# Two attention blocks over images: layer 1's first convolution taken in halves twice, and the projection put ahead of it

## The chip, the cores and the metric

The kernel runs on one core of a Trainium2 chip, all in float32. The metric is the device time of one launch in microseconds (us). The kernel before was timed in three runs; a further run was profiled. TensorE (PE in the profile) multiplies matrices, VectorE (DVE) and GpSimd (POOL) do elementwise work, ScalarE (ACT) does exponentials, copies and additions of a bias, and SyncE (SP) starts nearly all transfers (DMAs). On-chip data lie in SBUF; matrix products land in banks of PSUM.

## The reference

Input x has 8 images of 512 channels and 32 x 32 points (1024 tokens). Two layers follow each other, each adding its result to its input:

```
layer 0:  h = group_norm(x)                     (32 groups)
          q, k, v = W_qkv h + b_qkv             (8 heads of 64 channels)
          a = softmax(q k^T / 8) v              per head, over 1024 tokens
          x = x + W_proj a + b_proj             (called "projection", p)
layer 1:  h = group_norm(x)                     (8 groups)
          out = softmax((q h)(k h)^T / sqrt(512)) (v h)    one head
          x = x + W_p out + b_p
```

In layer 1 the kernel folds weights: the scores become g times h with g = m h plus a bias (m joins the weights of query and key), and the output becomes z = h times (value and projection weights joined), so layer 1 is g, scores, z, values. Dividing by the sum of exponentials is done afterwards, by a row of reciprocals r.

## The kernel before, in words

Everything is done image by image. An image of the steady loop (b from 1 to 6) passes these stages: layer 0's attention of image b; g of image b-1 and the projection of image b; layer 1's scores, z and values of image b-1; then v, k and q of image b+1. The matmuls stay in the order in which the program issues them, so the order of calls in the main loop is the order on TensorE. On the other engines a scheduler orders the instructions, except where `tc.keep_in_program_order` pins one.

**Products by halves.** `wino` splits both operands into halves and takes 7 products in place of 8, with sums of the factors made before (`left_sums` for the left operand, `right_sums` for the right one, where the image stands; `image_factors` calls the latter, 8 subtractions of 128x512). Each of the seven is a step of 4 matmuls of 128x128 by 512 columns (two parts of the output by two parts of the input channels; the profile counts each matmul twice, so it shows x8). `ORDER` is 1, 5, 2, 6, 7, 3, 4, while `middle` sets the order of the four steps between the first and the last two. Steps 1 and 2 add up in PSUM bank a, 6, 7 and 4 in bank b, 5 and 3 in bank c. The last two steps of a product are put in the list `tail`, and `finish()` issues them once the next product's first step has been issued; `hooks` are calls after the steps, and `background` is a list of small jobs of which each step takes some.

**Halves twice.** `conv2` applies the same splitting once more: 49 products of 128x128 by 256 columns instead of 28 by 512. Its operand needs `inner_factors`: 28 subtractions of 128x256 on GpSimd (line 411). Its weights are kept as `sums2_k` and `sums2_q` by `keep2`, which needs four additions of 128x896 on GpSimd (line 306), and are loaded in two parts. In before k and q of layer 0 are made by `conv2`; g (weights m), p, v and z by `wino`.

**Attention of layer 0.** `attention0` takes 8 blocks, each a pair of heads (`hp`, four of them) and a half of the tokens (`tb`). A block makes eight tiles of scores (`sc`), exponentials of them on ScalarE (`e`, line 594), their running sum on VectorE (lines 596 and 598), the values (`av`), then the sums over tokens by TensorE and their reciprocals by VectorE (`reciprocals`, line 559); a transfer spreads these over the partitions as r, and GpSimd multiplies (line 615). Only the last block's multiplication (line 617) is left for later, as `scaled`, on VectorE. `extra` holds 16 lists of jobs, two for each block: one between scores and values, one after the values. The images' normalisation (`h`, by ScalarE) is put there.

**g and the projection.** `layer1_scores` makes the factors of h on VectorE (lines 170 to 173), then g; `projection` follows, whose `residual` (lines 845 and 847) adds the bias and the input x, and puts statistics for layer 1's normalisation in the background. After the projection x is written to a spill buffer in DRAM. The attention's result a needs factors too: eight subtractions by `image_factors`, once the last block is scaled.

The following lines are those that a sentence can't say well: in before, the last block and the order of the main loop are

```
if (hp, tb) != (KC - 1, 1):
    nc.gpsimd.tensor_tensor(dst, dst, r, ALU.mult)
else:
    scaled = lambda dst=dst, r=r: nc.vector.tensor_mul(dst, dst, r)
...
hf, gf = layer1_scores(b - 1, h, ends)
norm1 = projection(b, af, xt)
```

Of the kernel before, what the change touches and what calls it, by code (L numbers as in the profile page):

```python
# [9 lines left out]
F32 = mybir.dt.float32  # L10
# [19 lines left out]
def two_attention_blocks_kernel(  # L30
# [145 lines left out]
    def main_path(ctx):  # L176
# [116 lines left out]

        wdram2 = {n: dram.tile([P, 7, 7, P], F32, name=f"sums2_{n}") for n in "qk"}

# [13 lines left out]

        twice = [("k", 0), ("k", 1), ("q", 0), ("q", 1)]  # L310
        uses = ["v", "p", *twice] if B > 1 else ["p"]
        for b in range(1, B):
            uses += ["m", "p", "z"] + (["v", *twice] if b + 1 < B else [])
        uses += ["m", "z"]
        loaded = []

        def load_weight():
            if uses:
                n = uses.pop(0)
                t = wpool.tile([P, 7 * C], F32, tag="w", name=f"w_{n[0]}_{len(uses)}")  # L320
                if n in twice:
                    t = t.rearrange("p (i j m) -> p i j m", i=4, j=7)
                    i = n[1]
                    t = t[:, : 4 - i]
                    nc.sync.dma_start(t, wdram2[n[0]][:, 4 * i : 4 + 3 * i])
                else:
                    t = t.rearrange("p (i k m) -> p i k m", i=7, k=2)
                    nc.sync.dma_start(t, wdram[n])
                loaded.append((n, t))
# [9 lines left out]

        def image_factors(h, uid):  # L340

            tiles = [pair_tile(f"t{i}_{uid}") for i in (1, 2, 4)]
            halves = lambda t: (t[:, :HT], t[:, HT:])
            return right_sums(
                [halves(t) for t in h[:2]], [halves(t) for t in h[2:]],
                [lambda j, t=t: t[:, j, :] for t in tiles], nc.vector.tensor_sub,
            )
# [67 lines left out]

        def conv2(n, f, bias, name, hooks=(), late=None):

# [121 lines left out]
            pair(2, (7,), [(1, 0)], [(0, 1)], [lambda: biased_half(1, 1)])  # L539
            last = [lambda: biased_half(0, 1), lambda: biased_half(1, 0)]  # L540
            if late is not None:
                late += last
                last = []
            pair(3, (3, 4), [(0, 1), (1, 0)], [(0, 1), (1, 0)], [load_weight, *last])
            return out


        def reciprocals(total, uid, across):

            sums = acc_tile(f"sums_{uid}")[:, : 2 * P].rearrange("p (a b) -> p a b", a=2)
            for i in range(4):
                matmul(sums[ts(i, 32), :, :], ones[:, :32], total[:, :, ts(i, P)], start=True, stop=True)
            rc = rpool.tile([P, 2, P], F32, tag="rc", name=f"rc_{uid}")
            nc.vector.reciprocal(rc, sums)  # L559
            nc.vector.tensor_tensor(low_recs, low_recs, rc, ALU.min)  # L560
            nc.gpsimd.tensor_tensor(all_recs, all_recs, rc, ALU.add)  # L561
            rows = rowpool.tile([2, 4, P], F32, tag="rows", name=f"rows_{uid}")
            nc.sync.dma_start(rows.rearrange("j i n -> i j n"), rc[0:P:32, :, :])
            if across:
                r = pair_tile(f"r_{uid}")
                for j in range(2):
                    row = rows[j : j + 1].rearrange("j i n -> j (i n)")
                    nc.sync.dma_start(r[:, j, :], row.to_broadcast([P, HT]))
            else:
                r = rpool.tile([P, HT], F32, tag="r", name=f"r_{uid}")  # L570
                for j in range(2):
                    row = rows[j : j + 1].rearrange("j i n -> j (i n)")
                    nc.sync.dma_start(r[ts(j, 64), :], row.to_broadcast([64, HT]))
            return r


        def attention0(b, q, k, v, extra):
            a = channel_tiles(f"a0_{b}")
            n = 0
            for hp in range(KC):  # L580
                for tb in range(2):
                    uid = f"0_{b}_{hp}_{tb}"
# [29 lines left out]
                    nc.scalar.copy(dst, av)  # L612
                    r = reciprocals(total, uid, False)
                    if (hp, tb) != (KC - 1, 1):
                        nc.gpsimd.tensor_tensor(dst, dst, r, ALU.mult)  # L615
                    else:
                        scaled = lambda dst=dst, r=r: nc.vector.tensor_mul(dst, dst, r)

            assert not extra
            return a, scaled  # L620

# [130 lines left out]
        def prologue():  # L752
# [44 lines left out]
            later = []  # L797
            for n in "pmz":
                t, steps = prepare(n)
                later.append(steps)  # L800
                later.append([lambda n=n, t=t: keep(n, t), load_weight])
            later.append([
# [3 lines left out]
            ])  # L806
            return v, q, k, norm1, later

        psum_pools("first", 2)
        v, q, k, norm0, later = prologue()  # L810

# [21 lines left out]

        def attention_steps(a, scaled, b):
            af, steps = image_factors(a, f"a_{b}")
            return af, [[], [scaled, lambda: background.extend(steps)]]

        def projection(b, af, xt):

            norm = GroupNorm(1, f"1_{b}")  # L840

            def residual(i, r, c, ps, u):
                oc = 2 * r + i
                xh = xt[oc][:, ts(c, HT)]
                nc.vector.scalar_tensor_tensor(xh, ps, obias[0][:, oc : oc + 1], xh, ALU.add, ALU.add)
                if u is not None:
                    nc.vector.tensor_add(xh, xh, u)  # L847
                background.append(lambda: norm.half_stats(oc, c, xh))

                if c == 1 - r:  # L850
                    background.append(lambda: norm.end_stats(oc))

            def store():
                spills[b] = spool.tile([KC, P, T], F32, tag="spill", name=f"spill_{b}")
                for c in range(KC):
                    nc.sync.dma_start(spills[b][c], xt[c])

            by_channel(weight("p"), af, f"p_{b}", residual, after=[load_weight, store])
            return norm

        def norm_hooks(norm, uid):
            return [
                [], [], [all_background], [lambda: norm.group_mean(acc_tile(f"gmean_{uid}")[:, :KC])],
                [lambda: norm.affine(acc_tile(f"gvar_{uid}")[:, :KC])],
            ]
# [25 lines left out]

        def layer1_scores(b, h, hooks):
            hf, steps = image_factors(h, f"h1_{b}")
            background.extend(steps)
            g = conv(
                weight("m"), hf, ubias, f"g1_{b}", middle=(2, 5, 6, 7), hooks=hooks, back=4,
                after=[load_weight, lambda: background.extend(gsteps)],
            )
            stiles = [pair_tile(f"sg{i}_{b}") for i in (1, 2, 4)]
# [4 lines left out]
            )  # L904
            return hf, gf

        def layer1_rest(b, hf, gf, hooks, ahead):
            e, total, ef = scores1(b, gf, hf, f"1_{b}", hooks)
            state = {}
# [18 lines left out]
        for b in range(B):  # L928
# [11 lines left out]
            for i, f in enumerate(applies):  # L940
                extra[2 * i + 3].append(f)
            if b > 0:
                extra[0] += late
            psum_pools(f"attention_{b}", 1)
            a, scaled = attention0(b, q, k, v, extra)
            psum_pools(f"products_{b}", 2)
            xt = [load_x(b, c, "x") for c in range(KC)]
            af, ends = attention_steps(a, scaled, b)
            if b > 0:
                hf, gf = layer1_scores(b - 1, h, ends)  # L950
                norm1 = projection(b, af, xt)
                if b + 1 < B:
# [8 lines left out]
            elif B > 1:  # L961
                v, f, norm0 = values(1, h, ends)
                norm1 = projection(0, af, xt)
                q, k, late = keys_and_queries(1, f, norm0, norm_hooks(norm1, "1_0")[1:])
            else:
                for f in sum(ends, []):
                    f()
                all_background()
                norm1 = projection(0, af, xt)
                finish()  # L970
                for f in sum(norm_hooks(norm1, "1_0"), []):
                    f()
                h, loads, applies = begun(load_again, norm1, 0, "h1")
                for f in loads + applies:
                    f()
        hf, gf = layer1_scores(B - 1, h, ())
        layer1_rest(B - 1, hf, gf, (), ())
# [196 lines left out]
```

## Time and profile before

| what | value |
|---|---|
| times of three runs | 2908.39, 2902.1, 2906.97 us (median 2906.97) |
| the profiled run | 2902.66 us, span of the core 2900.9 us, granted clock of TensorE 0.999 |
| busy: TensorE, VectorE, ScalarE, GpSimd | 2886.5, 1932.5, 872.2, 468.9 us |
| one block of attention (from 773.34 to 787.99) | 14.65 us |
| a step of 128x512 products in g or p | about 3.44 us |

A line of a timeline gives the start, the time from there to the end of a run of like instructions, the engine, the line of the code, the operation, output and inputs by their names with sizes, and how many (x). In brackets stands how long the engine was idle before it and which instruction released it. A line of a group gives the number of instructions, then their total busy time in us and the mean of one in ns, and then the idle time before them. Busy TensorE means no more than that matmuls were in flight: their ends are modelled.

### The profile page before, as it was taken

Reading aid. Unit: us, or ns where it says so; the run is one execution under the profiler, and the core shown is the slowest. Engines: PE = TensorE matmul, PEld = TensorE weight load, DVE = VectorE, ACT = ScalarE, POOL = GpSimd, SP = SyncE. Lnnn points to the kernel's source line nnn. Section 1 sums busy time; section 2 is a strip of 40 time slices with the busy share of each in tenths; the row PEclk is TensorE's granted clock in tenths of the full one; section 3 lists DMA queues with packets and bytes.
Section 4 is the critical chain, followed back from the end, with each engine's and each line's share of the span. In section 5 each row is a group of like instructions: output and inputs, shape, how many; then the busy total and the mean of one; then the engine's idle time right before and its main releaser. Section 6 shows DMA issues by size and latency. Waiting matters only on the chain.

```text
span 2900.9 us, 29024 instructions
## 1 busy us (share of the span) xinstructions
PE 2886.5 (100%) x10838; PEld 1500.3 (52%) x10838; DVE 1932.5 (67%) x2613; ACT 872.2 (30%) x1117; POOL 468.9 (16%) x525
## 2 busy tenths in 40 slices
PE   9999999999999999999999999999999999999999
PEld 5435634565345653457434574346733458334544
DVE  5488687567766578665776557866577665776555
ACT  1251451214512055121551115411163112631110
POOL 3023210032200321003210122102121031110000
PEclk9999999999999999999999999999999999999999
DMA  8433403123122231222212232122411224011201
GB/s 277 153 137 109 159 19 110 72 103 132 34 98 92 95 113 48 84 92 105 107 48 80 92 135 77 48 80 99 154 55 44 80 103 151 26 59 65 94 1 66
DMA packets 84186, 267.97 MB, mean 92 GB/s; under 512 B 10371, under 2 KB 29891, under 8 KB 75974
## 3 DMA queue, kind: packets, MB, share of 16 engines
q1 hardware_dynamic: 83622, 265.89, 25.5%
q8 instruction: 87, 1.43, 0.2%
q14 instruction: 61, 0.50, 0.1%
q10 hardware_dynamic: 416, 0.16, 0.0%
HBM read 216.30 MB, written 49.72 MB: 92 GB/s over the span
## 4 chain that ended last, share of the span: by engine, by line
PE 98%; issue 1%; DVE 0%; POOL 0%; ACT 0%; DVEq 0%; POOLq 0%
PE sc L67 16%; PE av L67 15%; PE psb_sc L67 6%; PE psb_av L67 6%; PE psa_av L67 4%; PE psa_sc L67 4%; PE psc_av L67 4%; PE psc_sc L67 4%; PE psb_g L67 3%; PE psb_z L67 3%; PE psb_p L67 3%; PE psb_v L67 3%; PE psb_k L67 3%; PE psb_q L67 2%; PE psa_g L67 2%; PE psa_v L67 2%
## 5 line engine op out<-in xcount | busy, mean ns | idle before, releaser
L598 DVE TENSOR_TENSOR sum<-sum,e 128x1024 f32<-128x1024 f32 x384 | 518.6, 1351 | 40.4 <-DVE sum L598 0.5
L594 ACT ACTIVATE e<-sc 128x1024 f32<-128x1024 f32 x512 | 476.8, 1052 | 72.9 <-PE sc L67 72.9
L67 PE MATMUL sc<-q,k 64*128 64x512 f32 x2048 | 458.3, 596 | 0.0
L67 PE MATMUL av<-e,v 128*64 128x512 f32 x2048 | 453.6, 595 | 0.0
L67 PEld LDWEIGHTS sc<-q,k 64*128 64x128 f32 x2048 | 192.3, 186 | 239.3 <-ACT e L594 110.3
L67 PEld LDWEIGHTS av<-e,v 128*64 128x64 f32 x2048 | 141.4, 137 | 304.3 <-issue 302.3
L561 POOL TENSOR_TENSOR all_recs<-all_recs,rc 128x256 f32<-128x256 f32 x72 | 64.4, 894 | 880.2 <-DVE rc L559 880.2
L559 DVE RECIPROCAL rc<-sums 128x256 f32<-128x256 f32 x72 | 126.4, 1756 | 89.7 <-PE sums L67 87.4
L615 POOL TENSOR_TENSOR a<-a,r 128x512 f32<-128x512 f32 x56 | 109.5, 1955 | 274.0 <-DMA r<-rows 247.5
L646 ACT ACTIVATE e<-e 128x512 f32<-128x512 f32 x96 | 60.5, 630 | 232.7 <-DVE e L645 232.7
L612 ACT COPY a<-av 128x512 f32<-128x512 f32 x64 | 37.4, 585 | 305.2 <-PE av L67 305.2
L596 DVE TENSOR_TENSOR sum<-e,e 128x1024 f32<-128x1024 f32 x64 | 78.6, 1228 | 59.8 <-ACT e L594 59.8
L67 PE MATMUL psa_sc<-g,h 128*128 128x512 f32 x256 | 115.7, 594 | 0.0
L67 PE MATMUL psa_av<-e,z 128*128 128x512 f32 x256 | 113.3, 595 | 0.0
L128 POOL TENSOR_TENSOR rstd<-ve,mhalf 128x4 f32<-128x4 f32 x16 | 16.7, 1043 | 499.9 <-DVE ve L126 499.9
L140 ACT ACTIVATE h<-h,b,s 128x1024 f32<-128x1024 f32 x62 | 78.5, 1270 | 60.7 <-DMA h<-in_x 48.0
L67 PEld LDWEIGHTS psa_sc<-g,h 128*128 128x128 f32 x256 | 48.1, 190 | 57.9 <-issue 56.2
L67 PEld LDWEIGHTS psa_av<-e,z 128*128 128x128 f32 x256 | 48.0, 190 | 57.3 <-issue 55.4
L67 PE MATMUL psb_k<-inner_h,w_k 128*128 128x256 f32 x294 | 75.4, 383 | 0.0
L67 PE MATMUL psb_q<-inner_h,w_q 128*128 128x256 f32 x294 | 74.9, 383 | 0.0
L249 ACT COPY t_sc<-psa_sc 128x512 f32<-128x512 f32 x32 | 18.7, 585 | 181.7 <-DVE x L847 152.4
L444 POOL TENSOR_TENSOR k<-k,k 128x256 f32<-128x256 f32 x28 | 20.0, 727 | 291.0 <-DVE u_k L439 291.0
(304 smaller groups left out, 4580.8 us busy)
## 6 DMA issues: line engine op xcount, KB each, us to landing
x<-in_x SPq DMA_DIRECT2D x36, 512.0 KB
h<-in_x SPq DMA_DIRECT2D x32, 512.0 KB
r<-rows SPq DMA_DIRECT2D x128, 128.0 KB
spill<-x SPq DMA_DIRECT2D x32, 512.0 KB
h<-spill SPq DMA_DIRECT2D x32, 512.0 KB
x<-spill SPq DMA_DIRECT2D x32, 512.0 KB
out<-x SPq DMA_DIRECT2D x64, 256.0 KB
w_p<-sums_p SPq DMA_DIRECT2D x8, 1792.0 KB
```

Source lines behind the costliest of these rows:

```text
L67: tc.keep_in_program_order(nc.tensor.matmul(*args, **kw))
L140: tc.keep_in_program_order(nc.scalar.activation(dst, src, AF.Identity, bias=b, scale=s))
L249: nc.scalar.copy(t1[i], ps["a", i])
L444: nc.gpsimd.tensor_tensor(d, x, y, ALU.add)
L559: nc.vector.reciprocal(rc, sums)
L561: nc.gpsimd.tensor_tensor(all_recs, all_recs, rc, ALU.add)
L594: nc.scalar.activation(e, sc, AF.Exp, scale=(C // 8) ** -0.5)
L596: nc.vector.tensor_add(total, es[0], e)
L598: nc.vector.tensor_add(total, total, e)
L612: nc.scalar.copy(dst, av)
L615: nc.gpsimd.tensor_tensor(dst, dst, r, ALU.mult)
L646: nc.scalar.activation(dst, dst, AF.Exp, scale=scale)
```

## The change

It has six parts.

1. g of images 0 to 6 is made by `conv2` (49 products of 256 columns), as k and q are. Its weights are loaded in two parts from `sums2_m`; four more additions of 128x896 on GpSimd make them, once, in the first attention. The last image's g stays with `wino`.
2. In the steady loop the projection goes ahead of g, with its middle steps in the order 5, 6, 7, 2. The scaled multiplication and the last two factors of a (t4) go in a hook of its third step. The first image has no g at that place.
3. The last pair of heads takes its second half of tokens first, so that the last block is the first half of a's last tile, which only products 2 and 4 of the projection read. The transfers of its reciprocals are issued by ScalarE, and the multiplication by them is pinned on VectorE.
4. The eight factors of h for g are made during the attention (two each in `extra` 9 to 12), six of a's eight factors are pinned there as well (`extra` 13 and 15), and h is normalised in `extra` 1, 3, 5 and 7 in place of 3, 5, 7 and 9. The 28 inner factors of h are issued after the attention on GpSimd.
5. The residual is pinned on VectorE; its statistics go in the background only within g; the hooks of the normalisation come one step earlier; `finish()` puts g's last steps before the scores' first; and `conv2` adds the bias of the half (1,0) before that of (0,1).
6. In the prologue the weights are prepared in the order p, z, m, and one load of weights moves.

The core of the diff:

```diff
-        wdram2 = {n: dram.tile([P, 7, 7, P], F32, name=f"sums2_{n}") for n in "qk"}
+        wdram2 = {n: dram.tile([P, 7, 7, P], F32, name=f"sums2_{n}") for n in "qkm"}
...
-            last = [lambda: biased_half(0, 1), lambda: biased_half(1, 0)]
+            last = [lambda: biased_half(1, 0), lambda: biased_half(0, 1)]
...
-                for tb in range(2):
+                for tb in (0, 1) if hp < KC - 1 else (1, 0):
...
-                    r = reciprocals(total, uid, False)
-                    if (hp, tb) != (KC - 1, 1):
+                    last = (hp, tb) == (KC - 1, 0)
+                    r = reciprocals(total, uid, False, nc.scalar if last else nc.sync)
+                    if not last:
                         nc.gpsimd.tensor_tensor(dst, dst, r, ALU.mult)
                     else:
-                        scaled = lambda dst=dst, r=r: nc.vector.tensor_mul(dst, dst, r)
+                        scaled = lambda dst=dst, r=r: tc.keep_in_program_order(nc.vector.tensor_mul(dst, dst, r))
...
-            for n in "pmz":
+            for n in "pzm":
                 t, steps = prepare(n)
                 later.append(steps)
-                later.append([lambda n=n, t=t: keep(n, t), load_weight])
+                later.append([lambda n=n, t=t: keep(n, t)])
+            later[1].append(load_weight)
...
-            return v, q, k, norm1, later
+            return v, q, k, norm1, later, lambda: (keep2("m", t), load_weight())
...
-                nc.vector.scalar_tensor_tensor(xh, ps, obias[0][:, oc : oc + 1], xh, ALU.add, ALU.add)
+                tc.keep_in_program_order(
+                    nc.vector.scalar_tensor_tensor(xh, ps, obias[0][:, oc : oc + 1], xh, ALU.add, ALU.add)
+                )
                 if u is not None:
                     nc.vector.tensor_add(xh, xh, u)
-                background.append(lambda: norm.half_stats(oc, c, xh))
+                stats.append(lambda: norm.half_stats(oc, c, xh))
...
-            g = conv(
-                weight("m"), hf, ubias, f"g1_{b}", middle=(2, 5, 6, 7), hooks=hooks, back=4,
-                after=[load_weight, lambda: background.extend(gsteps)],
-            )
+            after = [lambda: background.extend(gsteps)]
+            if inner:
+                g = conv2("m", inner, ubias, f"g1_{b}", hooks, after)
+            else:
+                g = conv(weight("m"), hf, ubias, f"g1_{b}", middle=(2, 5, 6, 7), back=4, after=[load_weight, *after])
...
+            finish()
             e, total, ef = scores1(b, gf, hf, f"1_{b}", hooks)
...
             for i, f in enumerate(applies):
-                extra[2 * i + 3].append(f)
+                extra[2 * i + 1].append(f)
+            a = channel_tiles(f"a0_{b}")
+            af, steps = image_factors(a, f"a_{b}", lambda *t: tc.keep_in_program_order(nc.vector.tensor_sub(*t)))
+            extra[13] += steps[:2]
+            extra[15] += steps[2:6]
             if b > 0:
                 extra[0] += late
+                hf, sums = image_factors(h, f"h1_{b - 1}")
+                for i in range(4):
+                    extra[9 + i] += sums[2 * i : 2 * i + 2]
...
             if b > 0:
-                hf, gf = layer1_scores(b - 1, h, ends)
-                norm1 = projection(b, af, xt)
+                inner, sums2 = inner_factors(hf, f"h1_{b - 1}")
+                for f in sums2:
+                    f()
+                hooks = [[], [], [scaled, *steps[6:]]]
+                norm1, stats = projection(b, af, xt, middle=(5, 6, 7, 2), hooks=hooks)
+                gf = layer1_scores(b - 1, hf, inner, [[], [lambda: background.extend(stats)]])
...
             elif B > 1:
-                v, f, norm0 = values(1, h, ends)
-                norm1 = projection(0, af, xt)
+                more_later()
+                v, f, norm0 = values(1, h, [[], [scaled, lambda: background.extend(steps[6:])]])
+                norm1, stats = projection(0, af, xt)
+                load_weight()
...
```

## The prediction

> **What bounds the kernel now.** I read the busy shares first, then the chain that ended last, then the form groups of the products, and last the timelines of one steady image.
>
> ```profile
> span 2900.9 us, 29024 instructions
> ...
> PE 2886.5 (100%) x10838; PEld 1500.3 (52%) x10838; DVE 1932.5 (67%) x2613; ACT 872.2 (30%) x1117; POOL 468.9 (16%) x525
> ...
> PE 98%; issue 1%; DVE 0%; POOL 0%; ACT 0%; DVEq 0%; POOLq 0%
> ```
>
> TensorE is the bound: 98% of the chain. A change pays only by fewer matmul cycles, or by removing the few waits that are left; and any other engine that comes late shows up one for one. So the prices are those of matmuls, and how late VectorE may be. A block of layer 0's attention starts at 773.34:
>
> ```profile
> 773.34 7.14 PE L67 MATMUL sc<-q,k 64*128 64x512 f32 x32
> ...
> 777.87 8.75 DVE L598 TENSOR_TENSOR sum<-sum,e 128x1024 f32<-128x1024 f32 x6
> 780.67 2.21 POOL L615 TENSOR_TENSOR a<-a,r 128x512 f32<-128x512 f32 x1 [4.34 <-DMA r<-rows]
> ...
> 787.42 0.64 PE L67 MATMUL sums<-sum,ones 128*32 128x256 f32 x8
> ...
> 788.18 1.76 DVE L559 RECIPROCAL rc<-sums 128x256 f32<-128x256 f32 x1 [1.56 <-PE sums L67]
> ```
>
> The reader is to see the margin: a block takes 787.99 - 773.34 = 14.65 us, the last add of its exponentials ends at 777.87 + 8.75 = 786.62, and the sums that need it start at 787.42. VectorE is early by about 0.75 us, no more. Where GpSimd's L615 runs, one of the adds takes 2.1 instead of 1.2 us (six adds in 8.75 us, against 7.87 in block 2 of the first attention, where no L615 runs beside them).
>
> The products of g and p in the steady image:
>
> ```profile
> 813.05 3.60 PE L67 MATMUL psb_g<-t_h,w_m 128*128 128x512 f32 x8
> 816.64 3.79 PE L67 MATMUL psb_g<-h,w_m 128*128 128x512 f32 x8
> 820.26 3.60 PE L67 MATMUL psa_p<-a,w_p 128*128 128x512 f32 x8
> 823.70 3.60 PE L67 MATMUL psb_g<-t_h,w_m 128*128 128x512 f32 x8
> ...
> 1005.53 1.03 PE L67 MATMUL psc_k<-inner_h,w_k 128*128 128x256 f32 x4
> 1006.40 1.03 PE L67 MATMUL psb_k<-inner_h,w_k 128*128 128x256 f32 x4
> ```
>
> Undisturbed steps start 823.70 - 820.26 = 3.44 us apart (four products, so 0.858 each at 512 columns), those in halves twice 0.87 for two products (0.431 to 0.435 each at 256). The second and third lines come 0.16 and 0.19 late: the waits in the present order.
>
> **What the Trainium skill says.** "SBUF — State Buffer", section "Who interferes with whom": a VectorE instruction with two SBUF inputs contends with a GpSimd instruction that reads SBUF, the pair of ports is an exclusive lock, and the loser blocks for a whole instruction; one with at most one SBUF input isn't touched. The trace agrees:
>
> ```profile
> 955.72 0.69 DVE L238 TENSOR_TENSOR w_av<-psb_av,t_av 128x512 f32<-128x512 f32 x1 [2.74 <-PE psb_av L67]
> ...
> 957.17 1.22 DVE L686 TENSOR_TENSOR o<-o,r 128x512 f32<-128x512 f32 x1
> 958.42 1.10 DVE L688 SCALAR_TENSOR_TENSOR x<-o,obias,x 128x512 f32<-128x512 f32 x1
> ```
>
> ```profile
> 957.80 1.17 POOL L411 TENSOR_TENSOR inner_h<-h 128x256 f32<-128x256 f32 x1
> ```
>
> L238 reads one input from PSUM and keeps its 0.69; L686 and L688 read two from SBUF while GpSimd forms factors, and take 1.22 and 1.10 instead of 0.69 and 0.75. So a VectorE instruction of that kind costs up to 0.5 us more whenever factors are formed beside it. The change puts 28 more of those on GpSimd per image.
>
> **Part 1, g in halves twice (images 0 to 6).** Removed: 28 products x 0.858 = 24.03 us. Added: 49 x 0.431 = 21.12. Gain 2.91 per image, 20.4 in all. k and q in the same form take 43.5 together against 42.2 by count, so each carries about 0.6 of waits of its own (0.1 to 0.2 at each of the later pairs); g's wait at its start is counted in part 2, so +0.5 here. The two weight loads of m instead of one lie on SP behind loads that are as large and are needed as late as k's; nothing waits for k's now, so nothing here.
>
> **Part 2, projection ahead of g.** The waits of the present mixture go: 0.16 + 0.19 + about 0.1 at g's start = -0.45. New: g's first product uses bank a, which the projection's second product fills last, and must wait until the residual (L845) has read it. Take T0 as the end of the attention's last sums. The projection's five steps end at T0 + 5 x 3.433 = 17.17. VectorE has in its fixed order ahead of that residual: last a*r (it can start at T0+11.2, behind two L238 adds of the product that ends at T0+10.3), two t4 subtractions, two L238, an L845, an L847, another L845, a statistics instruction, the other L847. At the spacings of 811 to 845 (0.60 for independent tensor_tensor, 0.66 for L845, 0.72 if it needs the one before) the residual ends at T0+18.06: TensorE waits 0.95 by the queue alone. GpSimd starts the 28 factor subtractions when the last scores are done (about T0-4.6; the pinned order lets them go no earlier), 0.68 each = 19 us, and 3 more with VectorE in the way: it is busy to T0+17 or beyond. a*r and the two L847 read two SBUF tiles: 3 x 0.25 = 0.75. I take 0.95 + 0.75 = 1.7; the ends are 0 (VectorE catches up) and 2.7 (every contested one, t4 as well, loses 0.35 to 0.5). The statistics that stand behind it in the queue are waited for by nobody for another 20 us.
>
> **Part 3, the last block with a's half that only two products need.** The scaled multiplication in before, at 811.68, was 9 us after the last sums; in the changed kernel T0+11.2 against a need at T0+13.7, so it is off the path with the 0.69 it takes; ACT issues its three transfers (rows and two broadcasts) instead of SP, between a's copy and the first copy of the projection, which has 3.4 us to spare. Nothing.
>
> **Part 4, factors spread over the attention.** VectorE gets two h subtractions in each of blocks 4, 5 and 6 between the sixth and the seventh add. In before the last add ends 13.28 after the block's start. Two subtractions of 0.60 come ahead of it, and as they need no add before them, two pauses of 0.1 between dependent adds (1.33 apart, 1.23 long) fall away: 13.28 + 1.2 - 0.2 = 14.28. The sums must start at 14.0 to keep the pace: 0.28 late per block, 0.84 per image (ends 0 and 1.2). Block 7 has GpSimd's factors beside its last three adds: it ends at 13.9 to 14.04, so 0 to 0.5; I take 0. The four a subtractions after it push its reciprocal to T0+1.7, which part 3's T0+11.2 includes. h's applies on ACT come one half-block earlier; their loads were issued by 676 and the first apply is due after 694. Nothing.
>
> **Part 5, statistics and the tail of g.** g's tail runs before the scores; ACT has two pairs of biased halves ahead of the first copy of the scores: four times 0.62 to 0.72, of which TensorE sees about 0.27 (ends 0 and 0.6).
>
> Per image: -2.91 + 0.5 - 0.45 + 1.7 + 0.84 + 0.27 = -0.05; times 7, -0.4.
>
> **Part 6, once.** m's four weight sums run on GpSimd in the first attention, from about 164.5: the same form in before,
>
> ```profile
> L306 POOL TENSOR_TENSOR prepare_k<-prepare_k 128x896 f32<-128x896 f32 x4 | 8.2, 2079 | 5.3 <-DMA sums_q<-prepare_q 5.3
> ```
>
> takes 2.08 us, read from SBUF throughout, against VectorE's chain of dependent adds with two SBUF inputs and 0.75 us of margin. Four locks of 1.95 over one or two blocks, less 0.75 in each: 3.6 to 5.8. I take 4. The first image has no g, only the better order: -0.3. The last image is as before: nothing.
>
> Sum: -0.4 + 4 - 0.3 = +3.3 on the profiled span of 2900.9. That span's run took 2902.66; the other three runs 2902.1, 2906.97 and 2908.39. On the median, 2906.97 + 3.3 = 2910. The likeliest case by itself lies at 2902 to 2919: part 2's wait at 1.0 and at 2.5 (times 7: -4.9 and +5.6), and about 3 for the spread of three runs.
>
> **Rivals.** (1) The matmuls' gain comes through: VectorE is nowhere late. Then -2.91 + 0.5 - 0.45 = -2.86 per image, -20 in all, 2887. For it: VectorE is busy 67% only, and a back-to-back burst of VectorE can keep GpSimd out instead. Against it: the 0.95 of part 2 needs no contention at all. (2) The order costs 0.95, GpSimd costs nothing in it: -0.80 x 7 + 4 - 0.3 = -1.9, 2905. (3) Slower: the port. If every two-input VectorE instruction ahead of the residual loses 0.35 or more (part 2 at 2.7) and block 7 ends 0.5 late, an image loses -0.05 + 1.0 + 0.5 = 1.45 us and, with 5.8 at once, the sum is 7 x 1.45 + 5.8 - 0.3 = +15.6, 2923. It decides (more than 5.8 us in all, with 4 at once) from where the two waits together exceed 2.05 us per image. For it: 1.22, 1.10 and 1.10 in the rows above. (4) The change does not do what it says: not possible for the products, whose number is fixed.
>
> **How the numbers follow.** Two medians of this kernel tell from no change about 0.2%, 5.8 us: below 2901 is faster, above 2913 slower. Likeliest case 0.50 (0.05 faster, 0.30 same, 0.15 slower); rival 1, 0.22 (0.20 faster, 0.02 same); rival 2, 0.08 (0.03, 0.05, 0); rival 3, 0.20 (slower). Faster 0.28, same 0.37, slower 0.35. Half of rival 1's chance lies below 2889 and half of rival 3's above 2922; the range is between.
>
> **What would show it.** Matmuls of g: 343 of 128x256 for seven images, PE busy less by about 20 us. Right: a gap before g's first product of 1 to 2.7 us that ends on L845's residual, gaps of 0.3 before the sums of blocks 4 to 6, and one-time gaps near 165 to 195. Wrong: no gap there (rival 1); VectorE's t4, L847 and a*r at 0.69 throughout refute the port; gaps in scores, z or k and q, which I hold for unchanged, would make it wrong by a cause that I have not priced.

## The result, and the profile after

The changed kernel takes 2920.3 us (median of 4 runs, 2919.5 to 2921.3) against 2904.5 before: ratio 1.0053, 95% interval 1.0036 to 1.0071. It is slower by about 16 us. The profiled spans are 2917.7 and 2900.9 us, a difference of 16.8, which the two traces can be made to add up to. Before's own runs mostly lie in two groups, near 2903 and near 2907 us, and its profile is of one in the first, so differences of medians and of spans agree only to within a few us.

First the page of the changed kernel, its span and busy times:

```profile
span 2917.7 us, 30228 instructions
...
PE 2881.4 (99%) x11132; PEld 1556.5 (53%) x11132; DVE 1995.8 (68%) x2753; ACT 923.0 (32%) x1201; POOL 706.2 (24%) x781
```

TensorE is busy 5 us less than before although the span is 17 longer: fewer matmul cycles, and new gaps. GpSimd is busy 237 us more. So I looked for TensorE's gaps, which before had hardly any. Of all waits of TensorE in one steady image (692 to 1050), the list of waits (those over 0.15 us; the total, how often, and the longest) gives one line, where the same stretch of before gives none:

```profile
PE psa_g L67 <- DVE x L847: 1.9, 1, 1.9
```

The place in TensorE's timeline, at the end of the projection's fifth step:

```profile
825.53 2.74 PE L67 MATMUL psa_p<-a,w_p 128*128 128x512 f32 x6
830.14 0.70 PE L67 MATMUL psa_g<-h,w_m 128*128 128x256 f32 x2 [1.87 <-DVE x L847]
830.68 0.59 PE L67 MATMUL psa_g<-t_h,w_m 128*128 128x256 f32 x2
831.11 5.29 PE L67 MATMUL psb_p<-t_a,w_p 128*128 128x512 f32 x8
836.24 2.31 PE L67 MATMUL psc_p<-a,w_p 128*128 128x512 f32 x5
```

Two things are to be seen. g's first product waits for the residual (L847 in this kernel's lines): from one matmul's start to the next 2.04 us more than the spacing. And the step behind it, eight instructions that took 3.43 us everywhere in before, takes 836.24 - 831.11 = 5.13: its matmuls start 0.853 apart in place of 0.429. The window view says why; its columns are the stretch, its length, TensorE's busy time and matmuls, the granted clock, and the share and rate of the transfers:

```profile
472.00:481.90 9.90, 8.03 (x21) 1.00 0.17 70
828.09:837.00 8.91, 7.04 (x15) 0.81 0.01 3
1185.00:1195.00 10.00, 8.14 (x22) 1.00 0.13 52
1541.00:1553.00 12.00, 10.12 (x22) 0.86 0.14 56
2255.00:2266.00 11.00, 9.13 (x20) 0.84 0.12 48
```

The same gap stands in all seven images; behind three of them (here 828, 1541 and 2255) the clock of TensorE is granted at half for about 3.4 us (8.91 x 0.19 / 0.5 in the second line), and 1.7 us are lost on top. Narrower windows bound the first of these stretches:

```profile
827.83:831.24 3.41, 1.54 (x7) 1.00 0.00 0
831.24:834.65 3.41, 3.41 (x6) 0.50 0.00 0
```

Which gaps are hit is not random. The trace's clock falls at 831.24, 1544.63 and 2258.01, 713.4 us apart, which is 209 times the 3.413 us that each half-speed stretch lasts. Divided into periods of that length from there, the trace has TensorE's idle time before g (about 1.87 us) wholly within one period in these three images. In the other four a boundary divides it, with at most 1.68 us in one period.

VectorE ahead of that residual:

```profile
822.12 0.68 DVE L619 TENSOR_TENSOR a<-a,r 128x512 f32<-128x512 f32 x1
822.71 2.35 DVE L949 TENSOR_TENSOR t_a<-a,t_a 128x512 f32<-128x512 f32 x2
...
829.35 1.40 DVE L847 SCALAR_TENSOR_TENSOR x<-psa_p,obias,x 128x512 f32<-128x512 f32 x2
```

The pair of t4 subtractions takes 2.35, where it took 1.28 in before:

```profile
816.50 1.28 DVE L173 TENSOR_TENSOR t_a<-a,t_a 128x512 f32<-128x512 f32 x2
```

The second place is a block of the attention. Two of h's subtractions stand ahead of the last add of a block, and the next sums start 780.74 - 765.87 = 14.87 us after these, in place of 14.65:

```profile
763.39 1.29 DVE L170 TENSOR_TENSOR t_h<-h 128x512 f32<-128x512 f32 x2
764.60 1.22 DVE L598 TENSOR_TENSOR sum<-sum,e 128x1024 f32<-128x1024 f32 x1
```

```profile
765.87 0.64 PE L67 MATMUL sums<-sum,ones 128*32 128x256 f32 x8
...
780.74 0.64 PE L67 MATMUL sums<-sum,ones 128*32 128x256 f32 x8
```

The third place comes once, in the first attention: GpSimd's four sums of m, VectorE's adds, and TensorE.

```profile
165.01 10.38 POOL L306 TENSOR_TENSOR prepare_m<-prepare_m 128x896 f32<-128x896 f32 x4 [5.02 <-DVE prepare_m L286]
```

```profile
167.31 3.10 DVE L596 TENSOR_TENSOR sum<-e,e 128x1024 f32<-128x1024 f32 x1
170.51 12.50 DVE L598 TENSOR_TENSOR sum<-sum,e 128x1024 f32<-128x1024 f32 x6
```

```profile
183.06 1.08 PE L67 MATMUL sums<-sum,ones 128*32 128x256 f32 x8 [5.29 <-DVE sum L598]
184.07 8.13 PE L67 MATMUL sc<-q,k 64*128 64x512 f32 x32
```

The seven adds of this block took 9.2 us in before:

```profile
167.34 1.23 DVE L596 TENSOR_TENSOR sum<-e,e 128x1024 f32<-128x1024 f32 x1 [0.74 <-ACT e L594]
168.67 7.87 DVE L598 TENSOR_TENSOR sum<-sum,e 128x1024 f32<-128x1024 f32 x6
```

Now they take 15.7, TensorE waits 5.3, and the scores behind it take 8.13 in place of 7.14: half clock again.

The sum of the differences, from the stages' starts in both traces: the first attention 124.03 against 117.23 (+6.8); the rest of the first image +0.55, its start -0.57; attention of images 1 to 7, 118.09 against 117.45 (+0.64 each, 4.5); the stage from the projection to the end of the scores +0.12 each where the clock stays whole and 1.7 more in three images (5.9), less 0.5 for waits that two images of before have of their own. That is 16.7 of the 16.8.

### The profile page after: what moved, and what is told of

It reads as the page before. It is cut to its first block, busy times and chain, and to the rows that moved or that the text cites. A ratio compares the mean times of both kernels' runs of the same rounds, so it can differ in the third digit from the quotient of the medians.

```text
span 2917.7 us, 30228 instructions
## 1 busy us (share of the span) xinstructions
PE 2881.4 (99%) x11132; PEld 1556.5 (53%) x11132; DVE 1995.8 (68%) x2753; ACT 923.0 (32%) x1201; POOL 706.2 (24%) x781
## 5 line engine op out<-in xcount | busy, mean ns | idle before, releaser
L598 DVE TENSOR_TENSOR sum<-sum,e 128x1024 f32<-128x1024 f32 x384 | 527.3, 1373 | 38.5 <-DVE sum L598 0.9
L411 POOL TENSOR_TENSOR inner_h<-h,inner_h 128x256 f32<-128x256 f32 x112 | 106.3, 954 | 0.5
L411 POOL TENSOR_TENSOR inner_h<-h 128x256 f32<-128x256 f32 x56 | 60.1, 1074 | 151.3 <-PE psc_av L67 151.3
L67 PE MATMUL psb_g<-inner_h,w_m 128*128 128x256 f32 x294 | 75.3, 383 | 0.0
```

Of the source, the lines that this page charges most:

```text
L67: tc.keep_in_program_order(nc.tensor.matmul(*args, **kw))
L411: nc.gpsimd.tensor_tensor(dst, x, y, ALU.subtract)
L598: nc.vector.tensor_add(total, total, e)
```

## The experiments

All times are medians; before took 2902 to 2910 in the same rounds, with a median of 2903 to 2907.

**m's sums pinned behind the attention.**

```diff
-                nc.gpsimd.tensor_tensor(dst, x, y, op)
+                i = nc.gpsimd.tensor_tensor(dst, x, y, op)
+                if n == "m":
+                    tc.keep_in_program_order(i)
```

> The changed kernel with one edit: the four sums of m's weights (128x896 on GpSimd) are pinned in program order, so that they run after the first attention and not beside its running sums. Theory (port): the 5.45 us gap in the first attention and the half-speed matmuls behind it go; the first attention takes 117.2 instead of 124.0 us, and the whole 6.8 us less than the changed kernel's 2920.3: about 2913.5. Rival (the cost only moves): GpSimd then has 8.2 us of sums ahead of the factors that k's products need, and the load of p's weights comes later; the products of the first image wait, and the gain is 0 to 3 us: 2917 to 2920.

Measured: 2921.3 us (1.0062 of before, 1.0046 to 1.0079). The first attention takes 117.23, as expected, so the sums were its trouble. But nothing was gained, as the rival has it: the cost moved. The list of waits of the first image's products reads

```profile
PE psb_v L67 <- DVE u_v L238: 3.5, 1, 3.5
PE psa_p L67 <- DMA w_p<-sums_p: 1.4, 1, 1.4
```

VectorE now loses the port on its factors for v (a pair of L172 takes 5.05 us in this trace), and the projection's weights are loaded late. Of the rival's two waits the second came; k's products, which it named first, don't wait.

**h's factors behind the last add.**

```diff
-                hf, sums = image_factors(h, f"h1_{b - 1}")
+                hf, sums = image_factors(h, f"h1_{b - 1}", lambda *t: tc.keep_in_program_order(nc.vector.tensor_sub(*t)))
                 for i in range(4):
-                    extra[9 + i] += sums[2 * i : 2 * i + 2]
+                    extra[7 + 2 * i] += sums[2 * i : 2 * i + 2]
```

> The changed kernel with one edit: h's factors on VectorE are pinned, two each behind the last add of blocks 3 to 6, in place of between the sixth and the seventh add of blocks 4 to 6. Theory (queue): the three gaps of 0.21 us before the sums go, 0.63 per image, 7 images: 4.4 us less than the changed kernel, 2916. Rival (VectorE is too full in any case): the later subtractions delay the reciprocal and with it the next block's first add, and gaps of the same size stay: 2920.

Measured: 2917.5 us (1.0046, 1.0029 to 1.0062), 2.8 under the changed kernel instead of 4.4. VectorE in block 4:

```profile
757.89 8.76 DVE L598 TENSOR_TENSOR sum<-sum,e 128x1024 f32<-128x1024 f32 x6
766.57 1.28 DVE L955 TENSOR_TENSOR t_h<-h,t_h 128x512 f32<-128x512 f32 x2
```

The adds end before the subtractions, and all 21 gaps of 0.21 are gone. In five of the seven images a new one of 0.3 to 0.45 comes before the sums of the last block, where GpSimd's factors run beside the adds: the edge that the prediction had set at 0 to 0.5. So the queue is shown, and a part of the rival with it.

**The residual of product 2 earlier.**

```diff
-                hooks = [[], [], [scaled, *steps[6:]]]
-                norm1, stats = projection(b, af, xt, middle=(5, 6, 7, 2), hooks=hooks)
+                hooks = [[], [scaled], steps[6:]]
+                norm1, stats = projection(b, af, xt, middle=(5, 6, 2, 7), hooks=hooks)
```

> The changed kernel with the projection's middle steps in the order 5, 6, 2, 7, the scaled multiplication pinned one step earlier, so that bank a is read a whole step before g's first product needs it. Theory: the gap of 2.04 us before g goes in all 7 images (14.3 us), and with it the half-speed matmuls that follow it in 3 of the 7 (1.7 us each, 5.1): 19.4 us less, 2901. Rival 1 (the wait moves to the reciprocals): product 2 now needs the scaled half at T0+10.3; if its row lands later than T0+9.5, a new wait of 1 us or more appears there: 2908 or more. Rival 2 (the half speed isn't caused by the gap): only 14.3 less, 2906.

Measured: 2911.4 us (1.0024, 1.0015 to 1.0034), 9 less than the changed kernel. The gap before g is gone in all images and no matmul of the stage runs at half speed, but rival 1 took its share:

```profile
823.53 2.84 PE L67 MATMUL psa_p<-a,w_p 128*128 128x512 f32 x6 [0.58 <-DVE a L619]
...
840.51 1.13 PE L67 MATMUL psb_g<-inner_h,w_m 128*128 128x256 f32 x4 [0.17 <-ACT u_g L481]
```

Product 2 waits 0.4 to 1.4 us for the scaled half, since the reciprocal stands behind four subtractions of a that GpSimd's factors slow down, and g's sixth step waits 0.2 more for a copy.

**TensorE kept busy in the gap.** Two products that nobody reads are put into the gap.

```diff
             if inner:
+                idle = acc_tile(f"idle_{b}")
+                for _ in range(2):
+                    matmul(idle, ident, hf[1][0], start=True, stop=True)
                 g = conv2("m", inner, ubias, f"g1_{b}", hooks, after)
```

> The changed kernel with two extra 128x512 products (1.72 us of matmuls, whose result nobody reads) ahead of g's first product, inside the gap of 2.04 us. They fit in the gap, so they cost nothing by themselves. Theory (TensorE's clock falls to half when the array has been idle): no half-speed matmuls behind the gap, 5.1 us less than the changed kernel where 3 of 7 gaps were followed by them, 2915. Rival (the projection's product 4 is slow because its operands or ports are contended): the slow matmuls stay, no difference, 2920.

Measured: 2915.7 us (1.0038, 1.0024 to 1.0052), 4.6 less, for more work. TensorE's timeline, and below it the window over the step behind the gap:

```profile
829.57 1.88 PE L67 MATMUL idle<-h,ident 128*128 128x512 f32 x4
831.61 0.70 PE L67 MATMUL psa_g<-h,w_m 128*128 128x256 f32 x2 [0.16 <-DVE x L847]
...
832.58 3.60 PE L67 MATMUL psb_p<-t_a,w_p 128*128 128x512 f32 x8
```

```profile
832.14:839.00 6.86, 6.86 (x18) 1.00 0.20 82
```

g starts no sooner, but the step behind it takes 3.43 us and the clock is whole, in all seven images. That TensorE's idle time, and no operand or port, halves the clock is shown. In the profiled run the three images gain the 5.1 us in full; its first attention is 1.4 longer, with half the clock for two periods instead of one.

**m's sums on VectorE.** `keep2_steps` is `keep2` for m, cut into its four sums, on VectorE and pinned:

```diff
+                tc.keep_in_program_order(nc.vector.tensor_tensor(dst, x, y, op))
...
+            later += [[m_steps[0]], [m_steps[1]], [], [m_steps[2]], [], [m_steps[3]]]
```

> The changed kernel with one edit: the four sums of m's weights are made by VectorE, one each behind the last add of blocks 3 to 6 of the first attention, in place of GpSimd in one run. Theory (port, and a place with slack): no VectorE add loses the port; the first attention takes 117.2 us as in before, and no new wait comes in the products behind it: 6.8 us less than the changed kernel, 2913.5. Rival: one sum of 896 elements takes about 1.05 us and delays the reciprocals, so a part of the gap stays: 2914 to 2919.

Measured: 2916.6 us (1.0038, 1.0024 to 1.0052), 3.7 less in place of 6.8. The first attention is at 117.23. What is missing is a wait of 3.2 us in v behind it:

```profile
PE psa_v L67 <- ACT t_v L249: 3.0, 1, 3.0
```

```profile
242.57 1.75 DVE L582 RECIPROCAL rc<-sums 128x256 f32<-128x256 f32 x1
```

ScalarE issues the transfers of the last reciprocals (part 3 of the change). Here the reciprocal comes 5 us into v, and the copies of v's first product stand behind the transfer that waits for it:

```profile
244.35 1.12 ACTq L586 DMA_DIRECT2D rows<-rc  x1
245.51 0.59 ACT L249 COPY t_v<-psa_v 128x512 f32<-128x512 f32 x1 [5.13 <-DVE t_h L171]
```

The releaser in brackets is only the one that came last by the profile; the copy starts when the transfer's issue ends. In all_mended below ScalarE issues the transfers too, but the reciprocal comes 0.2 us into v (238.67), and this wait is absent. So the rival's figure fits, but not its cause: no gap stays in the attention. The last three kernels below, which send it by SP in the first image, start v without that wait (17.37 us for its first steps, as in before).

**The order alone, g once by halves.** The sums of m go too, since nothing reads them; the rest of the change stays.

```diff
-            uses += ["p", *twice["m"], "z"] + ...
+            uses += ["p", "m", "z"] + ...
...
-                inner, sums2 = inner_factors(hf, f"h1_{b - 1}")
-                for f in sums2:
-                    f()
+                inner = None
```

> The changed kernel with g of all images made once by halves (28 products of 512 columns), so without inner factors on GpSimd and without m's sums; the order (projection first), the last block, the spread factors and the statistics stay. Theory: g costs 24.1 in place of 21.9 (+2.2 per image), the first attention is 6.8 shorter, the gap before g is 1.0 by the queue alone in place of 2.04 (-1.0), too short for half-speed matmuls (-5.1 in all), and the gaps of 0.21 in blocks 4 to 6 stay: 7 x 1.2 - 6.8 - 5.1 = -3.5 against the changed kernel, 2917, and 12 slower than before. Rival (the port does nothing): the gap before g stays at 2.0 and the half-speed matmuls with it: 2917 + 7 + 5 = 2929.

Measured: 2914.5 us (1.0031, 1.0018 to 1.0044). The gap before g is 0.92 in each image where the prediction's queue alone had 0.95, and its clock stays whole. One of the same t4 subtractions, and the residual:

```profile
817.59 0.69 DVE L949 TENSOR_TENSOR t_a<-a,t_a 128x512 f32<-128x512 f32 x1
...
822.50 1.40 DVE L847 SCALAR_TENSOR_TENSOR x<-psa_p,obias,x 128x512 f32<-128x512 f32 x2
```

Without factors on GpSimd t4 takes its own time. So 0.92 of the gap is the queue, and the other 1.1 goes with GpSimd's factors: the port. Without g in halves twice the rest of the change costs about 10 us.

**t4 behind the residual.**

```diff
-                hooks = [[], [], [scaled, *steps[6:]]]
+                hooks = [[], [], [scaled], [], steps[6:]]
```

> The changed kernel with one edit: the last two subtractions of a (t4) are pinned behind the residual that g's first product waits for. They took 2.35 us there, 1.3 by themselves and 1.06 for the port. Theory (queue plus port): the gap before g falls from 2.04 to about 0.3, a new one of up to 0.9 comes before the projection's product 4, which reads t4; no half-speed matmuls: -7 x 0.9 - 5.1 = -11 against the changed kernel, 2909. Rival (the queue is bound by its later members, not by t4): the gap stays at 1 or more, and with product 4's wait nothing is gained but the half speed: 2915 to 2920.

Measured: 2909.1 us (1.0013, 1.0006 to 1.0020), as the theory has it. The gap before g is 0.4 to 0.75 and the one before product 4 0.2 to 0.3, with 0.4 more inside product 4, between its matmuls; no half clock follows in any image.

**All mended, first try.** The edits of m_sums_vector, h_sums_behind and residual_early, and

```diff
-            extra[15] += steps[2:6]
             scaled = attention0(b, q, k, v, a, extra)
+            for f in steps[2:6]:
+                f()
...
-                        nc.gpsimd.tensor_tensor(dst, x, y, ALU.subtract)
+                        i = nc.gpsimd.tensor_tensor(dst, x, y, ALU.subtract)
+                        if pinned:
+                            tc.keep_in_program_order(i)
...
-            norm = GroupNorm(1, f"1_{b}")
+            norm = GroupNorm(1, f"1_{b}", True)
```

> The changed kernel with all waits taken away that were found: m's sums on VectorE; h's factors behind the last add; four of a's factors behind the last reciprocal; the projection's middle steps 5, 6, 2, 7 with the scaled multiplication a step earlier; the factors for g on GpSimd pinned behind the attention; the statistics pinned in g. Theory: what is left is the matmuls' gain: 2.2 per image less waits of some tenths, so 2904.5 - 7 x 2.0 = 2890. Rival (a wait moves in place of each that goes, GpSimd's factors now come late for g's later pairs): 2900 to 2910.

Measured: 2905.0 us (1.0005, 0.9996 to 1.0014): no difference from before. Attention (117.45) and projection have no wait left; g has three, and the first image's v and k 4 us of them. For one g (478 to 505):

```profile
PE psb_g L67 <- DVE u_g L464: 0.9, 1, 0.9
PE psc_g L67 <- DVE c_g L464: 0.6, 2, 0.4
```

Neither waits for an inner factor: VectorE's additions of g are late, with eight pinned statistics among them. The rival's waits came, by another cause than it named.

**Second try, and the same with g once by halves.** In mended_twice only four statistics are pinned, behind the last residual; in the first image a's factors wait for the projection, VectorE's scaled multiplication comes two steps later in v, and the transfers go by SP.

```diff
+            def first_stats():
+                norm.pinned = True
+                for f in stats[:4]:
+                    f()
+                del stats[:4]
+                norm.pinned = False
...
+            if b > 0:
+                for f in steps[2:6]:
+                    f()
...
-                v, f, norm0 = values(1, h, [[], [scaled, lambda: background.extend(steps[6:])]])
+                v, f, norm0 = values(1, h, [[], [], [], [scaled, lambda: background.extend(steps[2:])]])
...
-                    r = reciprocals(total, uid, False, nc.scalar if last else nc.sync)
+                    r = reciprocals(total, uid, False, nc.scalar if last and b > 0 else nc.sync)
```

> As all_mended, with what its trace showed mended too: the statistics are not pinned between g's additions, only the first four are, behind the last residual; in the first image a's factors wait for the projection instead of standing before v's additions, and its last reciprocals go by SP as in before. Theory (only VectorE's order kept TensorE waiting): the 2.0 us of waits in g per image and the 4 us in the first image's v and k go; the 15.4 us of g's halving twice come out: 2887 to 2890, 0.994 of before. Rival (GpSimd's factors, pinned behind the attention, are too late for g): g keeps waits of 1 us or more on inner factors, 2895 to 2900.

> As mended_twice, but g of all images made once by halves, with no inner factors for it and no sums of m. It tells what g in halves twice is worth by itself when nothing waits. Theory: 2.2 us per image by the matmuls (24.1 against 21.9 with k's and q's small waits), 15.4 in all, so 2903 where mended_twice is at 2888; and that 2903 is before's time, since the order alone brings nothing. Rival (the order and the early factors bring something of their own, waits of before that go): 2895 to 2900.

Measured: mended_twice 2900.4 us (0.9984, 0.9977 to 0.9991), mended_single 2906.9 us (1.0008, 1.0001 to 1.0015). From one attention's start to the next mended_single takes 355.17 us, and before 355.16: the order brings nothing of its own, as the theory has it. What mended_single loses it loses in the first image, 215.01 us against 209.79. mended_twice takes 354.17, with about 1 us of waits in g, behind four statistics in a row, and 5.5 us too much in the first image: 3.65 is a wait in v, 1.7 the half clock behind it. The cause of the wait is in VectorE's timeline, with GpSimd's beside it:

```profile
253.52 8.23 DVE L644 TENSOR_TENSOR a<-a,r 128x512 f32<-128x512 f32 x1
```

```profile
253.66 0.72 POOL L434 TENSOR_TENSOR inner_h<-h 128x256 f32<-128x256 f32 x1
254.34 0.71 POOL L434 TENSOR_TENSOR inner_h<-h,h 128x256 f32<-128x256 f32 x1
255.03 0.72 POOL L434 TENSOR_TENSOR inner_h<-h,inner_h 128x256 f32<-128x256 f32 x1
```

One multiplication of 0.69 us stands 8.23 us, while GpSimd forms factor after factor at its own pace.

**Third try.** Without `first_stats`; in the first image GpSimd does the multiplication itself, and the hook in v is two steps earlier again.

```diff
-                    if not last:
+                    scaled = lambda: None
+                    if not last or b == 0:
                         nc.gpsimd.tensor_tensor(dst, dst, r, ALU.mult)
```

> As mended_twice with two edits for what its trace shows. First, no statistics are pinned: the four behind the last residual held up an addition of g (0.86 and 0.21 us per image); unpinned they cost 0.33 in residual_early. Second, in the first image GpSimd multiplies the last block by its reciprocals, in its own queue among its factors, since VectorE's multiplication took 8.23 us there in place of 0.69 while GpSimd formed factors back to back, and TensorE waited 3.65 us for what was queued behind it. Theory (starved port, and VectorE's order): 0.7 less per image and 5.4 less at once, 2900.4 - 5.2 - 5.4 = 2890. Rival (the 8.23 us are a late transfer of r, not the port): GpSimd waits as long, the factors behind it come late for k, and only the 5.2 are gained: 2895.

Measured: 2890.0 us (2889.8 to 2890.2; 0.9945 of before, 0.9931 to 0.9959): as expected, and faster than both kernels.

```profile
span 2888.4 us, 30243 instructions
...
PE 2872.1 (99%) x11132; PEld 1555.7 (54%) x11132; DVE 1995.3 (69%) x2756; ACT 921.8 (32%) x1201; POOL 680.6 (24%) x778
```

```profile
247.19 1.27 POOL L643 TENSOR_TENSOR a<-a,r 128x512 f32<-128x512 f32 x1 [2.61 <-DMA r<-rows]
```

r is there at 247.2 here, 4 us after SP issued its transfers (243.2). In mended_twice SP issued them earlier:

```profile
242.31 1.81 SPq L598 DMA_DIRECT2D r<-rows  x2
```

So the 8.23 us at 253.5 were hardly a late transfer. An image takes 353.22 us, 1.95 less than mended_single, which has no wait in g: that is what g in halves twice is worth, 13.6 us in seven images. Its span is 12.5 below before's (2888.4 against 2900.9), not 13.6 or more, since the first image still loses 1.7, most of it in a wait of the projection for a's factors. Its engines are nearly as busy as the changed kernel's, and it is 30 us faster.

## Why the prediction was right or wrong

The range (2889 to 2922) holds the time, but the likeliest case (+3.3 us, with an upper end at 2919) does not: the kernel went to where the slower rival stood (+15.6). By its steps:

- **Part 1.** The count was right; the gain was mis-sized. g takes 21.92 in place of 24.14 us, 2.2 less, and 2.1 without the 0.1 of waiting at g's start that part 2 counts, not 2.91 - 0.5 = 2.4: conv2's own waits are 0.8.
- **Part 2, the waits of the present mixture** (-0.45): wrong. I read one image (2) and took it for all. Five of before's seven images take 100.14 us for the stage to the scores' end, and two have waits, of 0.34 and 0.16. Image 2 and image 1:

```profile
802.65:903.13 100.48, 100.48 (x248) 1.00 0.17 61
447.48:547.62 100.14, 100.14 (x249) 1.00 0.17 61
```

- **Part 2, the gap before g:** right in place and nearly in size, and in its two causes. 2.04 against 1.7; of it the queue 0.92 against 0.95 (order_alone), the port about 1.1 against 0.75. But the port hit t4, which the prediction had only in its upper end, and not a*r or the additions of the residual, on which it had put the 0.75.
- **Part 3** (nothing): right in the steady image, wrong for the first one: a transfer issued by ScalarE that waits holds ScalarE's copies. In the changed kernel v's first steps take 17.95 in place of 17.37 us, with a wait for the same copy; in m_sums_vector it was 3.2 us.
- **Part 4:** right, 0.21 per block against 0.28, 0.64 per image against 0.84.
- **Part 5:** 0.2 (the scores' stage lengthened from 48.23 to 48.43) against 0.27.
- **Part 6:** mis-sized: 6.8 against 4, above its upper end of 5.8, and the first image's 0.3 of recovery came out as nothing: its start is 0.57 earlier, and it loses 0.55 behind the attention. The four sums lengthened the seven adds of one block by 6.5 us in all, and half the clock came behind it.
- **What the sum lacked** is the largest single error of the steady images: that a gap can halve the clock behind it. It cost about 5 us in three images, and some 1 us in the first attention. The Trainium skill has it, in "TensorE: Matmul & The Clock Gate", Part 1 on the clock gate: the clock falls to half after an idle window of about 3.4 us, and the window runs freely, without regard to when a kernel starts. The runs agree on the half, on the length (3.41 us) and on a window that runs freely: it fits three of seven equal gaps being hit. But the window need not be idle throughout: 1.87 us of idle time in one was enough.

Over the whole kernel the errors are, in us: part 1 +2.0, the present waits +2.7, the gap +2.4, part 4 -1.4, part 5 -0.5, part 6 +2.8, the first image +0.3, the clock in three images +5.1. That is 13.4 of the 13.5 between the forecast (+3.3) and the spans (+16.8). The sign "PE busy less by about 20 us" came out as 5: matmuls at half clock count as busy for twice as long, and most of a wait of 0.21 is hidden under a matmul's modelled end.

The slower rival is right in its sum and only partly by its mechanism: it had the gap at 2.7 and block 7 at 0.5, which were 2.04 and 0; the clock filled the difference. That its sum fits is luck, and so in part is that the range, whose upper end rests on this rival, holds the time. What the change is after, 2.0 us per image, is real: mended_again has it.

## What to carry to other kernels

When TensorE is the bound, cost a change by the queues of the engines that feed it: list in order what stands ahead of the one instruction that TensorE waits for, and give two-input instructions of VectorE beside GpSimd's an upper price of about twice their own (2.35 for 1.28 here). Give a new gap of TensorE of 2 us its length plus a chance of the half-speed time behind it (1.7 us here, in 3 of 7). And read a wait of "the steady loop" in every turn of the loop, not in one.

## What the runs showed of the hardware that I had not expected

- A gap of 2.04 us in TensorE's work halved its clock for 3.41 us behind 3 of 7 gaps, and gaps of 0.92 and of 0.4 to 1.4 us behind none (order_alone, t4_behind, residual_early). Of the 28 gaps before g in the changed kernel, m_sums_after, h_sums_behind and m_sums_vector, 11 have their 1.87 to 2.00 us of idle time in one period of the 3.413 us grid, and just these are followed by half the clock; the other 17 have at most 1.84 in one. This isn't the whole rule: two gaps in the first image's v have 1.96 (m_sums_vector) and 1.89 us (mended_single) in one period, and no half clock behind them. Why is open. Four matmul instructions whose result nobody reads, in the gap, prevented it: 4.6 us less.
- One VectorE instruction of two SBUF inputs stood 8.23 us in place of 0.69 while GpSimd ran some eleven instructions back to back. "SBUF — State Buffer", section "Who interferes with whom", says that the loser blocks until the other's instruction is finished; here it lost again and again. In mended_single it stood 7.90 us at the same place. That each of GpSimd's instructions takes the lock anew ahead of VectorE is inferred from the two timelines.
